# A three-layer graph network with max aggregation on one core: five heavy units for six, distances on ScalarE, the leaky relu on GpSimd, and three middle tiles that pick an edge per pair of source tiles

## The chip, the cores and the metric

The kernel runs on one core of a Trainium2 chip. The time is device time in microseconds for one execution. The profile names the engines PE (TensorE), DVE (VectorE), ACT (ScalarE), POOL (GpSimd) and SP (SyncE, which only issues DMAs here); PEld is TensorE's weight load.

## The reference

`x` has 6250 rows of 128 values, and 200000 edges go from `src` to `dst`, sorted by `dst`. Low node numbers get many edges and high ones few, since `dst` is 6250 times the square of a uniform number. Three SAGE layers of widths 128, 256, 256 take the maximum over incoming edges:

```
def _sage_conv(x, src, dst, Wl, bl, Wr):
    agg = segment_max(x[src], dst, num_segments=x.shape[0])
    agg = where(isfinite(agg), agg, 0.0)
    return agg @ Wl + bl + x @ Wr

h = maximum(_layernorm(x), 0.0)
h = leaky_relu(_sage_conv(h, src, dst, Wl1, bl1, Wr1), 0.01)
h = leaky_relu(_sage_conv(h, src, dst, Wl2, bl2, Wr2), 0.01)
h = leaky_relu(_sage_conv(h, src, dst, Wl3, bl3, Wr3), 0.01)
out = x + h
```

## The kernel before, in words

Nodes are cut into 50 tiles of 127 rows, 25 pairs of source tiles. An edge is aggregated in one of two ways.

The first is a one-hot product. For a destination row and a pair of source tiles, one edge is picked, ScalarE makes a one-hot matrix from the row number (`one_hot`), and TensorE multiplies the pair's rows by it (`products`, line 1002), each row as two halves that add up to it. VectorE takes the maximum into `acc` (`maxima`, line 1026). A light unit ("n") picks one edge per pair, and its two source tiles go into one product and one maximum. The other units ("m", "w", and the heavy units' second set "x") pick one edge per source tile, which means two products and two maxima (the code calls such a step `alone`, or `odd`). A step is 1024 columns in layer 0 and 512 in layers 1 and 2. The units form five groups, each with a plane of 128 columns per unit: 24 light tiles, 11 middle tiles (11 to 21), the heavy rows (tiles 0 to 2, cut into `NV` units of rows with at most `CUT_V` edges, followed by their second set), 8 wide tiles and 4 more light ones. `STARTS` says at which pair of a layer each group enters; in layers 1 and 2 the light and the heavy group take part from pair 0 to 24, the middle one from 10 to 34, the wide one from 19, and the last four from 28.

The second way is for edges that are left over. They are sorted by list length, and `Listed.gather` fetches a row per list place by an indirect DMA on GpSimd (line 1064), followed by a pause, a `memset` of 300 columns (`gap_t`, line 1068). VectorE takes maxima over the gathered tiles (lines 1079 and 1084) some steps later. `CAPS` holds how long each list is.

What is picked is worked out in layer 0, beside its products. `expand` finds, for each row and each source tile, the smallest edge: five distances by an exclusive or (line 772), a tree of minima (line 778) and a reduction, all on VectorE. Each is one chore of `late_lookups`; the chores are spread over the steps of layer 0 by their cost.

When a tile's products and lists are done, `Node` runs it in stages on later steps: `fetch` (GpSimd, line 1118), `merge`, `linear` (TensorE into `z_p`, then ScalarE copies `z_p` to `s`, line 1151), `rows` (VectorE's leaky relu into `h`, lines 1158 and 1162, and the write to the next layer's table), `turn` (TensorE transposes `h` into `hT_p`, line 908; ScalarE rounds `h` into `pr`) and `rest` (`keep_halves`: VectorE subtracts, line 918). In layer 0 such a tile starts every step, in layer 1 and 2 every second step for the light and middle tiles.

The order is written out by hand: a loop over steps `t` issues what `agenda` holds for the step, in ranks. Each engine runs its instructions in that order.

Of the kernel before, what the change touches and what calls it, by code (L numbers as in the profile page):

```python
# [32 lines left out]
F32 = mybir.dt.float32  # L33
# [3 lines left out]
I16 = mybir.dt.int16  # L37
# [17 lines left out]
LEAF = 1 << 14  # L55
VT, NV, CUT_V = 3, 6, 96
CAPS = (
    (13, 11, 10, 9, 8, 8, 7, 7, 6, 6, 6, 6, 5, 5, 5, 4, 4, 4, 3, 3, 3, 2, 2, 1),
    (26, 22, 18, 13, 9, 5),
    (14, 11, 10, 8, 7, 7, 6, 5, 4, 4, 3),  # L60
    (33, 24, 20, 17, 15, 13, 11, 9),
    (14, 10, 8, 6),
)
# [7 lines left out]
FIRST = 24  # L71
PAUSE = 300


@with_exitstack
def kernel(ctx: ExitStack, tc: tile.TileContext, x, src, dst,
# [15 lines left out]
    widths = (D, H, H)  # L92
    PAST = NG << 8
    assert NT * P <= PAST and PAST + NT * P < LEAF


    WIDE = list(range(VT, 11))
    NARROW = list(range(26, NT)) + list(range(22, 26))
    MIDDLE = list(range(11, 22))
    NW, NN, NM = len(WIDE), len(NARROW), len(MIDDLE)  # L100
    VIRT = 2
    GROUPS = (
        [("n", i) for i in range(24)],
        [("m", i) for i in range(NM)],
        [("w", NW + v) for v in range(NV)],
# [426 lines left out]
    def flag_rows(us, S):  # L532
# [45 lines left out]
    def pick_rows(k, i0, us, S):  # L578
# [186 lines left out]

    def expand(us, J, g0, s, least, S):

        n = len(us)
        r = rows_of(us)
        t = S(0, I16, BATCH * n, J).rearrange("p (i u) j -> p i u j", i=BATCH)  # L770
        for i in range(BATCH):
            nc.vector.tensor_scalar(
                t[:, i, :, :], r[:, :, :J], ((g0 + i) << 8) | (s << 7), None, op0=OP.bitwise_xor
            )
        w = J
        while w % 4 == 0 and w > 8:
            w //= 2
            nc.vector.tensor_tensor(t[:, :, :, :w], t[:, :, :, :w], t[:, :, :, w : 2 * w], op=OP.min)
# [4 lines left out]
    turns = itertools.cycle(("tr", "z"))  # L783
    stored = [0] * len(GROUPS)

    def lookups(us, least, s, pool, tags=("v", "v8")):

        n = len(us)
        wide = us[0][0] != "n"
        v = pool.tile([P, n, NG], BF16, tag=tags[0], name="v", bufs=1 + (tags[0] == "v"))  # L790
        nc.vector.scalar_tensor_tensor(v, least, float(P if wide else 2 * P), least, op0=OP.is_lt, op1=OP.mult)
        v8 = pool.tile([NG, n * P], U8, tag=tags[1], name="v8")
        i = 0
        while i < n:
# [107 lines left out]
    def halves(layer, a, h):  # L902
# [11 lines left out]
        return pr  # L914

    def keep_halves(layer, a, h, pr):
        F = widths[layer]
        nc.vector.tensor_sub(pr[:, 1, :F], h[:, :F], pr[:, 0, :F].bitcast(F32))
        nc.sync.dma_start(pairs[layer][a // 2][:, a % 2, :, :], pr[:, :, :F].bitcast(F32))
# [109 lines left out]
    class Listed:  # L1029
# [25 lines left out]
        def gather(self, t):  # L1055
# [11 lines left out]
            )  # L1067
            nc.gpsimd.memset(gap_t, 0.0)  # L1068

# [30 lines left out]
    class Node:  # L1100
# [41 lines left out]
        def linear(self):  # L1142
# [7 lines left out]
            self.s = s = node.tile([P, H], F32, tag="s", name="s", bufs=2)  # L1150
            nc.scalar.copy(s[:R, :FO], z_p[:R, :])  # L1151

        def rows(self):
            layer, a, FO, s = self.layer, self.a, self.FO, self.s
            if layer < 2:
                self.h = h = h_ts[turn_h[0] % len(h_ts)]
                turn_h[0] += 1
                nc.vector.scalar_tensor_tensor(h[:R, :FO], s[:R, :FO], SLOPE, s[:R, :FO], op0=OP.mult, op1=OP.max)  # L1158
# [3 lines left out]
            nc.vector.scalar_tensor_tensor(s[:R, :FO], s[:R, :FO], SLOPE, s[:R, :FO], op0=OP.mult, op1=OP.max)  # L1162
# [124 lines left out]
    def late_lookups(us, s):  # L1287
        got = {}
        for g0 in range(0, NG, BATCH):
# [5 lines left out]
        chores.append((2, lambda: lookups(us, got[0], s, made)))  # L1295

# [478 lines left out]
```

## Time and profile before

| | us |
|---|---|
| runs, median of 3 | 3166.22 (3161.16 to 3170.59) |
| profiled execution | 3162.05 |
| its span, first to last instruction | 3160.2 |
| busy: VectorE | 2717.8 (86%) |
| busy: GpSimd | 2430.8 (77%) |
| busy: TensorE | 2332.1 (74%) |
| busy: ScalarE | 1433.9 (45%) |

A group of instructions in the profile is told as: line, engine, operation, output<-input, shapes, count | busy us, mean ns of one | idle us of the engine just before them <- what ended it. A wait is told as: who waited <- for what: us in total, times, longest. DMA-issuing and register instructions are not counted as busy, and "issue" is time in which an engine waited for nothing that the profile shows.

### The profile page before, as it was taken

Reading aid. Unit: us, or ns where it says so; the run is one execution under the profiler, and the core shown is the slowest. Engines: PE = TensorE matmul, PEld = TensorE weight load, DVE = VectorE, ACT = ScalarE, POOL = GpSimd, SP = SyncE. Lnnn points to the kernel's source line nnn. Section 1 sums busy time; section 2 is a strip of 40 time slices with the busy share of each in tenths; the row PEclk is TensorE's granted clock in tenths of the full one; section 3 lists DMA queues with packets and bytes.
Section 4 is the critical chain, followed back from the end, with each engine's and each line's share of the span. In section 5 each row is a group of like instructions: output and inputs, shape, how many; then the busy total and the mean of one; then the engine's idle time right before and its main releaser. Section 6 shows DMA issues by size and latency. Waiting matters only on the chain.

```text
span 3160.2 us, 37328 instructions
## 1 busy us (share of the span) xinstructions
PE 2332.1 (74%) x9394; PEld 1710.8 (54%) x9394; DVE 2717.8 (86%) x4441; ACT 1433.9 (45%) x2394; POOL 2430.8 (77%) x3424
## 2 busy tenths in 40 slices
PE   1024554456566778899888878889999988888997
PEld 1023333334344455677666656666676666666665
DVE  6668988987898975999999988876799999998995
ACT  5214443333544666555454434444555545443342
POOL 6666888688778883888888786763688888788882
PEclk9996766777767999999999999999999999999998
DMA  9322334266645797556454456778455554555675
GB/s 259 116 65 82 116 111 115 80 179 215 197 156 174 221 270 243 160 157 189 144 153 151 149 162 217 235 217 265 155 172 162 174 141 156 157 153 174 201 221 153
DMA packets 303458, 538.58 MB, mean 170 GB/s; under 512 B 57245, under 2 KB 165589, under 8 KB 302595
## 3 DMA queue, kind: packets, MB, share of 16 engines
q1 hardware_dynamic: 206573, 302.97, 29.7%
q0 software_dynamic: 78592, 196.07, 23.0%
q10 hardware_dynamic: 18070, 37.07, 3.1%
q8 instruction: 79, 1.29, 0.2%
q14 instruction: 144, 1.18, 0.1%
HBM read 409.84 MB, written 126.04 MB: 170 GB/s over the span
## 4 chain that ended last, share of the span: by engine, by line
DVE 19%; PE 16%; POOL 12%; DMA 6%; issue 6%; ACT 1%; SPq 0%; DVEq 0%; POOLq 0%; ACTq 0%
DVE acc L1026 13%; PE pg L1002 11%; POOL g L1064 8%; DMA g<-table,let 4%; POOL gap_t L1068 3%; DVE g L1079 2%; DVE g L1084 2%; PE z_p L1147 2%; PE z_p L1149 1%; DMA out_dram<-s 1%; DMA pair_sb<-pair 1%; ACT hot L985 0%; DMA agg_v<-best,end_i 0%; PE hT_p L908 0%; DMA xt<-in_x_dram 0%
## 5 line engine op out<-in xcount | busy, mean ns | idle before, releaser
L1002 PE MATMUL pg<-hot,pair_sb 128*128 128x512 f32 (+1 forms) x7500 | 2036.3, 421 | 414.2 <-DVE acc L1026 241.3
L1002 PEld LDWEIGHTS pg<-hot,pair_sb 128*128 128x128 f32 x7500 | 1436.1, 202 | 873.4 <-issue 285.9
L1064 POOL DMA_INDIRECT g<-table,let x1518 | 1523.9, 1004 | 492.6 <-issue 237.6
L1026 DVE TENSOR_TENSOR acc<-acc,pg 128x1024 f32<-128x1024 f32 (+4 forms) x1614 | 1663.6, 1057 | 207.1 <-PE pg L1002 164.7
L985 ACT ACTIVATE hot<-idx_sb 128x1024 fp32r<-128x1024 uint8 (+2 forms) x1050 | 909.6, 886 | 714.0 <-PE pg L1002 548.5
L1068 POOL MEMSET gap_t<- 128x300 f32 x1518 | 566.5, 373 | 0.7
L983 ACT ACTIVATE hot<-idx_sb,last_b 128x1024 fp32r<-128x1024 int8 (+1 forms) x300 | 310.3, 1034 | 37.2 <-PE pg L1002 24.9
L1118 POOL DMA_INDIRECT agg<-best,end_i x141 | 140.1, 994 | 104.1 <-PE aT_p L1134 60.5
L1151 ACT COPY s<-z_p 127x256 f32<-127x256 f32 (+1 forms) x150 | 50.4, 336 | 363.2 <-PE z_p L1149 325.8
L1079 DVE TENSOR_TENSOR g<-g 128x1024 f32<-128x1024 f32 (+6 forms) x214 | 207.8, 971 | 0.3
L1084 DVE TENSOR_TENSOR g<-g 128x256 f32<-128x256 f32 (+3 forms) x377 | 183.2, 487 | 11.2 <-issue 0.2
L1147 PE MATMUL z_p<-wr,hT_in 128*128 128x256 f32 (+1 forms) x500 | 138.7, 395 | 0.6 <-DMA hT_in<-across 0.6
L1149 PE MATMUL z_p<-wl,mz 128*128 128x256 f32 (+1 forms) x500 | 121.4, 360 | 11.9 <-DVE mz L1140 11.9
L908 PE MATMUL hT_p<-ident,h 128*128 128x128 f32 x200 | 44.3, 306 | 88.2 <-DVE h L1158 82.0
L973 DVE TENSOR_SCALAR idx_sb<-idx_sb,own_b 128x512 int32<-128x512 int32 (+3 forms) x125 | 73.4, 588 | 35.8 <-DMA idx_sb<-idx 30.6
L910 ACT COPY hT<-hT_p 128x254 f32<-128x254 f32 x100 | 37.1, 371 | 145.8 <-PE hT_p L908 129.0
L1149 PEld LDWEIGHTS z_p<-wl,mz 128*128 128x128 f32 x500 | 89.5, 204 | 25.1 <-DVE mz L1140 14.9
L652 POOL DMA_INDIRECT picks<-picked,to_i x53 | 61.5, 1161 | 48.2 <-DVE rank_f L629 23.5
L1140 DVE TENSOR_TENSOR mz<-acc,aT_p 128x256 f32<-128x256 f32 (+1 forms) x141 | 52.4, 371 | 53.3 <-PE aT_p L1134 53.3
L1147 PEld LDWEIGHTS z_p<-wr,hT_in 128*128 128x128 f32 x500 | 80.7, 203 | 31.7 <-issue 13.3
L908 PEld LDWEIGHTS hT_p<-ident,h 128*128 128x128 f32 x200 | 24.1, 149 | 120.1 <-issue 54.9
L806 ACT CAST v<-lk_p 25x1024 uint8<-25x1024 bf16 (+4 forms) x16 | 11.5, 747 | 165.7 <-PE lk_p L804 165.7
(291 smaller groups left out, 1298.0 us busy)
## 6 DMA issues: line engine op xcount, KB each, us to landing
pair_sb<-pair SPq DMA_DIRECT2D x106, 512.0 KB
idx_sb<-far SPq DMA_DIRECT2D x100, 384.0 KB
pair<-pr SPq DMA_DIRECT2D x100, 256.0 KB
g<-table,let POOLq DMA_INDIRECT x1518
pair_sb<-pair SPq DMA_DIRECT2D x85, 256.0 KB
idx_sb<-idx SPq DMA_DIRECT2D x50, 384.0 KB
far<-idx_sb ACTq DMA_DIRECT2D x50, 384.0 KB
idx_sb<-far SPq DMA_DIRECT2D x50, 352.0 KB
```

The lines of the kernel that those rows point to most:

```text
L973: nc.vector.tensor_scalar(words, words, own_b.bitcast(I32)[:, 0:1], None, op0=OP.bitwise_xor)
L983: nc.scalar.activation(hot[:, :w], far_b.bitcast(I8), AF.Relu, bias=last_b, scale=-1.0)
L985: nc.scalar.activation(hot[:, :w], far_b, AF.Relu, bias=1.0, scale=-1.0)
L1002: nc.tensor.matmul(to, pr[:, s, i, kk * P : (kk + 1) * P], hot[:, o : o + bw], start=((alone or s == 0) and i == 0), stop=((alone or s == ...
L1026: nc.vector.tensor_max(to, to, of)
L1064: nc.gpsimd.indirect_dma_start(out=self.tiles[q, b][:, i, :], out_offset=None, in_=tables[self.layer], in_offset=bass.IndirectOffsetOnAxis ...
L1068: nc.gpsimd.memset(gap_t, 0.0)
L1079: nc.vector.tensor_max(base[:, : i + 1, :], base[:, : i + 1, :], g[:, : i + 1, :])
L1084: nc.vector.tensor_max(base[:, :h, :], base[:, :h, :], base[:, w - h : w, :])
L1118: nc.gpsimd.indirect_dma_start(out=self.agg[:, : self.F], out_offset=None, in_=of, in_offset=bass.IndirectOffsetOnAxis(ap=at, axis=0),)
L1147: nc.tensor.matmul(z_p, self.hT[:, i, :], wr[layer][:, i, :], start=False, stop=False)
L1149: nc.tensor.matmul(z_p, self.m[:, i, :], wl[layer][:, i, :], start=False, stop=(i == K - 1))
```

## The change

- The heavy rows form five units of up to 104 edges instead of six of up to 96, so their plane has 10 places instead of 12.
- Tiles 19 to 21 become light units that stay in the middle group's plane, behind its other eight.
- A source node's number becomes 256 x tile + row (it was 128 x tile + row in effect, as node number plus tile). For all but light units the five distances are then ScalarE's `Abs` with a bias (`keys`), issued one chore ahead of the minima, in four scratch areas in turn. Light units keep VectorE's exclusive or. Two small operations per pick bring the number back.
- `CAPS` holds other list lengths, 487 places in all instead of 490.
- ScalarE computes relu(z) into `s` and relu(-0.01 z) into `h`, and GpSimd subtracts them (`in_place`). The subtraction of `keep_halves` is GpSimd's too. For each of these, the next two gathers go without their pause.

The diff, cut to its core:

```diff
+FAR = 2 * P
-VT, NV, CUT_V = 3, 6, 96
+VT, NV, CUT_V = 3, 5, 104
 CAPS = (
-    (13, 11, 10, 9, 8, 8, 7, 7, 6, 6, 6, 6, 5, 5, 5, 4, 4, 4, 3, 3, 3, 2, 2, 1),
...
+    (13, 11, 10, 9, 8, 8, 7, 7, 6, 6, 6, 5, 5, 5, 4, 4, 4, 4, 3, 3, 2, 2, 1, 1),
...
+SPARE = 2
-    NARROW = list(range(26, NT)) + list(range(22, 26))
-    MIDDLE = list(range(11, 22))
+    NARROW = list(range(26, NT)) + list(range(22, 26)) + list(range(19, 22))
+    MIDDLE = list(range(11, 19))
...
-        [("m", i) for i in range(NM)],
+        [("m", i) for i in range(NM)] + [("n", i) for i in range(28, NN)],
...
-    nc.vector.scalar_tensor_tensor(scol, c_i, 1.0, srci, op0=OP.add, op1=OP.add)
+    nc.vector.tensor_scalar(c_i, c_i, float(FAR - R), 1.0, op0=OP.mult, op1=OP.add)
+    nc.vector.tensor_tensor(scol, c_i, srci, op=OP.add)
...
-        nc.vector.tensor_scalar(picked[k][:, i0 : i0 + n, :], top, -float(LEAF), 0.0, op0=OP.add, op1=OP.max)
+        pick, off = picked[k][:, i0 : i0 + n, :], S(1, I16, n, m)
+        nc.vector.tensor_scalar(pick, top, -float(LEAF), 0.0, op0=OP.add, op1=OP.max)
+        nc.vector.tensor_scalar(off, pick, 1.0 / FAR, -0.499, op0=OP.mult, op1=OP.add)
+        nc.vector.scalar_tensor_tensor(pick, off, -float(FAR - P), pick, op0=OP.mult, op1=OP.add)
...
-    def expand(us, J, g0, s, least, S):
+    def expand(us, J, g0, s, S, area=0):
         n = len(us)
         r = rows_of(us)
-        t = S(0, I16, BATCH * n, J).rearrange("p (i u) j -> p i u j", i=BATCH)
+        wide = us[0][0] != "n"
+        t = S(area, I16, BATCH * n, J).rearrange("p (i u) j -> p i u j", i=BATCH)
         for i in range(BATCH):
-            nc.vector.tensor_scalar(
-                t[:, i, :, :], r[:, :, :J], ((g0 + i) << 8) | (s << 7), None, op0=OP.bitwise_xor
-            )
+            a = 2 * (g0 + i) + s
+            if wide:
+                nc.scalar.activation(t[:, i, :, :], r[:, :, :J], AF.Abs, bias=keys[:, a : a + 1], scale=1.0)
+            else:
+                nc.vector.tensor_scalar(t[:, i, :, :], r[:, :, :J], a * FAR, None, op0=OP.bitwise_xor)
+        return t
+
+    def shrink(t, us, J, g0, least):
...
+    paused = [0]
+
+    def in_place(out, a, b):
+        nc.gpsimd.tensor_tensor(out, a, b, op=OP.subtract)
+        paused[0] += SPARE
+
     def keep_halves(layer, a, h, pr):
         F = widths[layer]
-        nc.vector.tensor_sub(pr[:, 1, :F], h[:, :F], pr[:, 0, :F].bitcast(F32))
+        in_place(pr[:, 1, :F], h[:, :F], pr[:, 0, :F].bitcast(F32))
...
-            nc.gpsimd.memset(gap_t, 0.0)
+            if paused[0]:
+                paused[0] -= 1
+            else:
+                nc.gpsimd.memset(gap_t, 0.0)
...
-            nc.scalar.copy(s[:R, :FO], z_p[:R, :])
+            self.h = b = h_ts[turn_h[0] % len(h_ts)]
+            turn_h[0] += 1
+            nc.scalar.activation(s[:R, :FO], z_p[:R, :], AF.Relu)
+            nc.scalar.activation(b[:R, :FO], z_p[:R, :], AF.Relu, scale=-SLOPE)
...
-                nc.vector.scalar_tensor_tensor(h[:R, :FO], s[:R, :FO], SLOPE, s[:R, :FO], op0=OP.mult, op1=OP.max)
+                in_place(h[:R, :FO], s[:R, :FO], h[:R, :FO])
...
-            nc.vector.scalar_tensor_tensor(s[:R, :FO], s[:R, :FO], SLOPE, s[:R, :FO], op0=OP.mult, op1=OP.max)
+            in_place(s[:R, :FO], s[:R, :FO], h[:R, :FO])
...
                 if g0 == 0:
-                    got[0] = made.tile([P, len(us), NG], I16, tag="least", name="least", bufs=2)
-                expand(us, slots_of(us), g0, s, got[0], S_acc)
+                    got["least"] = made.tile([P, len(us), NG], I16, tag="least", name="least", bufs=2)
+                    got[0] = expand(us, J, 0, s, S_acc, next(areas))
+                if g0 + BATCH < NG:
+                    got[g0 + BATCH] = expand(us, J, g0 + BATCH, s, S_acc, next(areas))
+                shrink(got.pop(g0), us, J, g0, got["least"])
...
-        late_lookups(GROUPS[1], s)
+        late_lookups(GROUPS[1][:NM], s)
+    late_lookups(GROUPS[1][NM:], 0)
```

Three places show how instructions move. The first is VectorE's queue in layer 1, one pair of source tiles in which the light, the middle and the heavy group take part (`acc_1500` and `acc_1505` hold the light group, `acc_1501` and `acc_1506` the others). Before:

```order
L1026 TENSOR_TENSOR acc_1501<-acc_1501,pg 128x2x512 x5
L1026 TENSOR_TENSOR acc_1501<-acc_1501,pg 128x2x256 x4
L1026 TENSOR_TENSOR acc_1500<-acc_1500,pg 128x2x512 x2
L1026 TENSOR_TENSOR acc_1501<-acc_1501,pg 128x2x384
L1079 TENSOR_TENSOR g<-g 128x1024
L1026 TENSOR_TENSOR acc_1501<-acc_1501,pg 128x2x384
L1026 TENSOR_TENSOR acc_1501<-acc_1501,pg 128x2x512 x2
```

The same place in the changed kernel:

```order
L1054 TENSOR_TENSOR acc_1506<-acc_1506,pg 128x2x512
L1054 TENSOR_TENSOR acc_1506<-acc_1506,pg 128x2x128
L1054 TENSOR_TENSOR acc_1506<-acc_1506,pg 128x2x384
L1054 TENSOR_TENSOR acc_1506<-acc_1506,pg 128x2x128
L1054 TENSOR_TENSOR acc_1506<-acc_1506,pg 128x2x384
L1054 TENSOR_TENSOR acc_1505<-acc_1505,pg 128x2x512
L1110 TENSOR_TENSOR g<-g 128x1024
L1054 TENSOR_TENSOR acc_1505<-acc_1505,pg 128x2x512
L1054 TENSOR_TENSOR acc_1506<-acc_1506,pg 128x2x384
L1054 TENSOR_TENSOR acc_1506<-acc_1506,pg 128x2x256 x2
```

The three tiles' 384 columns come once instead of twice, and the heavy group's last maxima are 2x256 instead of 2x512; its other part splits as 128 and 384 instead of 256 and 256.

The second is VectorE's queue in layer 0, one chore that looks up the heavy units. Before, with the distances (L772) ahead of the tree:

```order
L772 TENSOR_SCALAR acc_1500<-rows_w 128x576 x5
L778 TENSOR_TENSOR acc_1500<-acc_1500 128x30x48
L778 TENSOR_TENSOR acc_1500<-acc_1500 128x30x24
L778 TENSOR_TENSOR acc_1500<-acc_1500 128x30x12
L778 TENSOR_TENSOR acc_1500<-acc_1500 128x30x6
L779 TENSOR_REDUCE least<-acc_1500 128x5x6
```

In the changed kernel the distances stand on ScalarE's queue, between one-hots (L1011, L1013) and the numbers for gathers (L1081):

```order
L1470 DMA far_158<-idx_sb 128x3072
L783 ACTIVATE acc_1505<-rows_w,keys 128x520 x10
L1011 ACTIVATE hot<-idx_sb,last_b 128x1024
L1081 ACTIVATE let<-ell_852 128x1
L1013 ACTIVATE hot<-idx_sb 128x1024
L783 ACTIVATE acc_1506<-rows_w,keys 128x520 x5
```

and VectorE's queue has, for the first of these chores:

```order
L1001 TENSOR_SCALAR idx_sb<-idx_sb,own_b 128x768
L793 TENSOR_TENSOR acc_1505<-acc_1505 128x25x52
L793 TENSOR_TENSOR acc_1505<-acc_1505 128x25x26
L794 TENSOR_REDUCE least<-acc_1505 128x5x5
L1115 TENSOR_TENSOR g<-g 128x384
```

Five distances and two minima left VectorE's queue per chore; the first lookup of a kind puts ten distances in a row on ScalarE's.

The third is GpSimd's queue in layer 0 while a tile's stages run each step. Before:

```order
L1118 DMA agg<-best_0_140,end_i_861 128x128
L1064 DMA g<-table_75,let 128x128
L1068 MEMSET gap_t 128x300
L1064 DMA g<-table_75,let 128x128
L1068 MEMSET gap_t 128x300
L1064 DMA g<-table_75,let 128x128
L1068 MEMSET gap_t 128x300
```

In the changed kernel:

```order
L1149 DMA agg<-best_0_140,end_i_862 128x128
L941 TENSOR_TENSOR h_1484<-s,h_1484 127x256
L941 TENSOR_TENSOR pr<-h_1483,pr 128x256
L1092 DMA g<-table_75,let 128x128 x3
L1149 DMA agg<-best_0_140,end_i_862 128x128
```

The pauses are gone and two subtractions stand ahead of the step's gathers. In layer 0, 130 gathers go without a pause; the first 70 gathers of layer 1 and the first 82 of layer 2 do so too, on what the layer before left over.

More of the change, by code (lines that the diff above doesn't have):

```diff
@@ L55 @@
 LEAF = 1 << 14
-VT, NV, CUT_V = 3, 6, 96
+VT, NV, CUT_V = 3, 5, 104
 CAPS = (
-    (13, 11, 10, 9, 8, 8, 7, 7, 6, 6, 6, 6, 5, 5, 5, 4, 4, 4, 3, 3, 3, 2, 2, 1),
[L59 to L62, printed above, removed]
+    (13, 11, 10, 9, 8, 8, 7, 7, 6, 6, 6, 5, 5, 5, 4, 4, 4, 4, 3, 3, 2, 2, 1, 1),
+    (29, 23, 18, 13, 9),
+    (16, 12, 11, 10, 9, 8, 7, 6, 5, 5, 3),
+    (30, 23, 19, 16, 14, 12, 10, 8),
+    (14, 10, 8, 5),
 )
@@ L92 @@
     widths = (D, H, H)
-    PAST = NG << 8
-    assert NT * P <= PAST and PAST + NT * P < LEAF
+    PAST = NG * 2 * FAR
+    assert NT * FAR <= PAST < LEAF and LEAF + PAST < 1 << 15
     WIDE = list(range(VT, 11))
-    NARROW = list(range(26, NT)) + list(range(22, 26))
-    MIDDLE = list(range(11, 22))
+    NARROW = list(range(26, NT)) + list(range(22, 26)) + list(range(19, 22))
+    MIDDLE = list(range(11, 19))
     NW, NN, NM = len(WIDE), len(NARROW), len(MIDDLE)
@@ L109 @@
     EXTRA = [("x", v) for v in range(NV)]
-    PLANES = [units + (EXTRA[4:] + EXTRA[:4] if k == VIRT else []) for k, units in enumerate(GROUPS)]
+    EC = (2 * NV) % 4
+    assert 4 < NV < 8 and 2 * NV - EC == 8
+    PLANES = [units + (EXTRA[EC:] + EXTRA[:EC] if k == VIRT else []) for k, units in enumerate(GROUPS)]
     STARTS = ((0, 40, 25, 53, 60), (0, 10, 0, 19, 28), (0, 10, 0, 19, 28))
@@ L541, in flag_rows @@
             nc.vector.tensor_copy(ri, r[:, :, :J])
-            nc.vector.tensor_scalar(g, ri, 8, None, op0=OP.arith_shift_right)
+            nc.vector.tensor_scalar(g, ri, 9, None, op0=OP.arith_shift_right)
             nc.vector.tensor_tensor(b, one[:, None, :].to_broadcast([P, n, J]), g, op=OP.logical_shift_left)
-            nc.vector.tensor_scalar(o, ri, 24, 31, op0=OP.logical_shift_left, op1=OP.arith_shift_right)
+            nc.vector.tensor_scalar(o, ri, 23, 31, op0=OP.logical_shift_left, op1=OP.arith_shift_right)
             nc.vector.tensor_tensor(o, o, b, op=OP.bitwise_and)
@@ L552, in flag_rows @@
             g, seen = (S(i, I32, n, J) for i in (1, 1))
-            nc.vector.tensor_scalar(g, r[:, :, :J], 1.0 / 256, -0.499, op0=OP.mult, op1=OP.add)
+            nc.vector.tensor_scalar(g, r[:, :, :J], 1.0 / (2 * FAR), -0.499, op0=OP.mult, op1=OP.add)
             nc.vector.tensor_tensor(b, one[:, None, :].to_broadcast([P, n, J]), g, op=OP.logical_shift_left)
@@ L783 @@
     turns = itertools.cycle(("tr", "z"))
+    areas = itertools.cycle(range(4))
+    keys = keep.tile([P, NT], F32, name="keys")
+    nc.vector.tensor_scalar(keys, iota_f[:, :NT], -float(FAR), None, op0=OP.mult)
     stored = [0] * len(GROUPS)
@@ L789, in lookups @@
         wide = us[0][0] != "n"
+        if not wide:
+            less = pool.tile([P, n, NG], I16, tag=tags[0] + "_less", name="less")
+            nc.vector.tensor_scalar(less, least, float(FAR), float(P - FAR), op0=OP.is_ge, op1=OP.mult)
+            nc.vector.tensor_add(least, least, less)
         v = pool.tile([P, n, NG], BF16, tag=tags[0], name="v", bufs=1 + (tags[0] == "v"))
@@ L799, in lookups @@
             if us[i] in EXTRA:
-                m = min(m, 4 - us[i][1] % 4)
+                m = min(m, (EC if us[i][1] < EC else NV) - us[i][1])
             at = PLANES[k].index(us[i]) + (len(PLANES[k]) if s else 0)
@@ L886 @@
     for g0 in range(0, NG, BATCH):
-        expand(L0, CB, g0, 0, least, S_first)
+        shrink(expand(L0, CB, g0, 0, S_first), L0, CB, g0, least)
     next(rest_v, None)
@@ L1150, in linear @@
             self.s = s = node.tile([P, H], F32, tag="s", name="s", bufs=2)
-            nc.scalar.copy(s[:R, :FO], z_p[:R, :])
+            self.h = b = h_ts[turn_h[0] % len(h_ts)]
+            turn_h[0] += 1
+            nc.scalar.activation(s[:R, :FO], z_p[:R, :], AF.Relu)
+            nc.scalar.activation(b[:R, :FO], z_p[:R, :], AF.Relu, scale=-SLOPE)
         def rows(self):
-            layer, a, FO, s = self.layer, self.a, self.FO, self.s
+            layer, a, FO, s, h = self.layer, self.a, self.FO, self.s, self.h
             if layer < 2:
-                self.h = h = h_ts[turn_h[0] % len(h_ts)]
-                turn_h[0] += 1
-                nc.vector.scalar_tensor_tensor(h[:R, :FO], s[:R, :FO], SLOPE, s[:R, :FO], op0=OP.mult, op1=OP.max)
+                in_place(h[:R, :FO], s[:R, :FO], h[:R, :FO])
                 nc.sync.dma_start(tables[layer + 1][1 + a * P : 1 + (a + 1) * P, :], h)
@@ L1270, in late_rows @@
         i0 = 0
-        for part in (us,):
+        for _, part in itertools.groupby(us, key=lambda u: u[0]):
+            part = list(part)
             chores.append((2.5, lambda part=part: mask_rows(part, S_acc)))
@@ L1288, in late_lookups @@
         got = {}
+        J = slots_of(us)
         for g0 in range(0, NG, BATCH):
@@ L1291, in part @@
                 if g0 == 0:
-                    got[0] = made.tile([P, len(us), NG], I16, tag="least", name="least", bufs=2)
-                expand(us, slots_of(us), g0, s, got[0], S_acc)
+                    got["least"] = made.tile([P, len(us), NG], I16, tag="least", name="least", bufs=2)
[3 more added lines that the diff above has]
+                shrink(got.pop(g0), us, J, g0, got["least"])
             chores.append((.7 * len(us), part))
-        chores.append((2, lambda: lookups(us, got[0], s, made)))
+        chores.append((2, lambda: lookups(us, got["least"], s, made)))
     stops = []
```

## The prediction

> **What bounds the kernel now.** I read the page's first lines, then the busy times by stage, then who waits for whom inside the long stages, and last the groups of instructions by form.
>
> ```profile
> span 3160.2 us, 37328 instructions
> PE 2332.1 (74%) x9394; PEld 1710.8 (54%) x9394; DVE 2717.8 (86%) x4441; ACT 1433.9 (45%) x2394; POOL 2430.8 (77%) x3424
> ```
>
> No engine fills the span, so the average decides nothing. The cut into stages does (stretch and its length, then busy us of PE, PEld, DVE, ACT and POOL with instruction counts, then the granted clock, DMA share and GB/s):
>
> ```profile
> 0.00:229.00 229.00, 31.70 (x140) 25.31 (x140) 149.13 (x618) 62.48 (x143) 146.65 (x168) 1.00 0.49 142
> 229.00:402.00 173.00, 87.49 (x284) 65.35 (x284) 156.98 (x398) 80.17 (x107) 131.50 (x193) 0.73 0.34 104
> 402.00:629.00 227.00, 110.03 (x351) 81.28 (x352) 206.34 (x476) 88.32 (x124) 184.90 (x267) 0.70 0.37 105
> 629.00:822.00 193.00, 116.68 (x396) 76.49 (x394) 159.06 (x336) 73.01 (x158) 161.01 (x224) 0.76 0.65 198
> 822.00:986.00 164.00, 103.43 (x298) 70.88 (x298) 152.55 (x323) 77.82 (x127) 131.50 (x188) 0.72 0.56 168
> 986.00:1216.00 230.00, 170.78 (x611) 111.50 (x609) 182.63 (x292) 137.68 (x243) 179.69 (x250) 0.88 0.78 233
> 1216.00:1850.00 634.00, 568.31 (x2319) 422.62 (x2320) 581.00 (x639) 331.33 (x493) 522.35 (x765) 0.98 0.53 163
> 1850.00:2201.00 351.00, 302.29 (x1342) 227.42 (x1341) 276.86 (x355) 142.59 (x298) 225.90 (x306) 0.97 0.71 223
> 2201.00:2835.00 634.00, 571.77 (x2338) 423.37 (x2337) 581.42 (x634) 330.54 (x488) 522.27 (x766) 0.99 0.52 160
> 2835.00:3160.00 325.00, 269.61 (x1324) 206.60 (x1322) 271.79 (x378) 109.91 (x218) 225.07 (x304) 0.93 0.63 189
> ```
>
> The first row is the setup, the next five are layer 0, then come layers 1 and 2, each cut where the 24 light tiles' matmuls end (1850, 2835). VectorE is the fullest engine in layer 0 until 986, except from 629 to 822, and in the long halves of layers 1 and 2 (581 of 634 us, 92%). After 1850 TensorE is (302 of 351). GpSimd looks free and is not: half its instructions are gathers, and each costs issue time that is not counted as busy.
>
> ```profile
> L1064 POOL DMA_INDIRECT g<-table,let x1518 | 1523.9, 1004 | 492.6 <-issue 237.6 <-ACT let L1053 162.5 <-DMA across<-hT 27.6
> L1068 POOL MEMSET gap_t<- 128x300 f32 x1518 | 566.5, 373 | 0.7
> L1118 POOL DMA_INDIRECT agg<-best,end_i x141 | 140.1, 994 | 104.1 <-PE aT_p L1134 60.5 <-issue 16.0 <-DMA pair_sb<-pair 11.1
> ```
>
> A gather with its pause costs 1.00 + 0.37 + 237.6/1518 = 1.53 us. The 380 of 1216 to 1850 take 582 of 634 us. With the 27.6 us wait for the table at a layer's start, GpSimd has about 25 us to spare there. So VectorE is first, GpSimd close behind, TensorE third (568). The waits from 1264 to 1820 agree:
>
> ```profile
> PE pg L1002 <- DVE acc L1026: 44.0, 61, 2.4
> POOL g L1064 <- ACT let L1053: 12.2, 8, 7.6
> DVE acc L1026 <- PE pg L1002: 11.7, 19, 1.9
> ```
>
> TensorE waits four times as long for the maxima as VectorE for the products, and GpSimd hardly waits.
>
> **The change, part by part.** VectorE's rows:
>
> ```profile
> L1026 DVE TENSOR_TENSOR acc<-acc,pg 128x1024 f32<-128x1024 f32 x1096 | 1305.9, 1216 | 149.3 <-PE pg L1002 123.5 <-ACT acc L1024 4.4 <-ACT hot L985 1.3
> L1026 DVE TENSOR_TENSOR acc<-acc,pg 128x512 f32<-128x512 f32 x272 | 186.0, 684 | 15.8 <-PE pg L1002 5.6 <-ACT acc L1024 2.5
> L1026 DVE TENSOR_TENSOR acc<-acc,pg 128x768 f32<-128x768 f32 x147 | 139.7, 950 | 38.0 <-PE pg L1002 35.0
> L1026 DVE TENSOR_TENSOR acc<-acc,pg 128x384 f32<-128x384 f32 x49 | 26.9, 550 | 2.5 <-PE pg L1002 0.7
> L1026 DVE TENSOR_TENSOR acc<-acc,pg 128x256 f32<-128x256 f32 x50 | 21.0, 420 | 1.7
> L1158 DVE SCALAR_TENSOR_TENSOR h<-s 127x256 f32<-127x256 f32 x100 | 42.1, 421 | 8.8 <-ACT s L1151 4.9 <-DMA table<-h 3.8
> L918 DVE TENSOR_TENSOR pr<-h,pr 128x256 fp32r<-128x256 f32 x100 | 42.0, 420 | 14.0 <-ACT pr L913 13.8
> L1162 DVE SCALAR_TENSOR_TENSOR s<-s 127x128 f32<-127x128 f32 x50 | 14.3, 286 | 6.3 <-ACT s L1151 6.2
> L772 DVE TENSOR_SCALAR acc<-rows_x 128x576 int16<-128x576 int16 x50 | 19.7, 458 | 0.0
> L772 DVE TENSOR_SCALAR acc<-rows_w 128x512 int16<-128x512 int16 x50 | 19.7, 456 | 0.0
> L772 DVE TENSOR_SCALAR acc<-rows_w 128x576 int16<-128x576 int16 x50 | 19.3, 449 | 0.0
> L772 DVE TENSOR_SCALAR acc<-rows_m 128x528 int16<-128x528 int16 x50 | 17.6, 417 | 0.0
> L778 DVE TENSOR_TENSOR acc<-acc 128x660 int16<-128x660 int16 (+7 forms) x150 | 77.6, 518 | 5.2
> ```
>
> Five heavy units: the plane of heavy units has 10 places instead of 12, so its second part is 2 units wide instead of 4. In layers 1 and 2 that makes 50 maxima of 1024 elements into 512: 50 x (1.216 - 0.684) = 26.6 us a layer; in layer 0, 50 x (0.684 - 0.420) = 13.2. The first part only splits elsewhere. TensorE saves half of 200 matmuls a layer, at 568.31/2319 = 0.245 us each: 24 us.
>
> Pair tiles 19 to 21: their product is one maximum instead of two, 25 fewer a layer: 25 x 0.950 = 23.8 us in layers 1 and 2, 15 x 0.950 = 14 of it before 1850 (2835); 25 x 0.550 = 13.8 in layer 0. TensorE does the same matmuls.
>
> Distances: 76.3 us of L772 leave VectorE in layer 0 (those of the heavy units, 39.0, before 629; the others, 17.6 and 19.7, mostly from there to 822 and half of the last after it). The tree under them loses 30 of 150 instructions of 0.52 us. Against that, the three tiles' own distances stay on VectorE, and each of the ten pick blocks gains two small operations. I set these equal: zero.
>
> Counted lists: 503 gathers a layer instead of 506, under 5 us of GpSimd each: zero.
>
> Relu on GpSimd: 98.4 us leave VectorE (L1158, L918, L1162). GpSimd gets 250 subtractions, and skips the pause of two gathers for each; 485 of 500 skips find a gather. The trace has no GpSimd instruction with two inputs, so I bound it by `gap_t`'s row above and these two:
>
> ```profile
> masks.py:199 POOL TENSOR_SCALAR_AFFINE_SELECT ident<-ident 128x128 f32<-128x128 f32 x1 | 0.3, 292 | 0.1
> masks.py:197 POOL MEMSET ident<- 128x128 f32 x1 | 0.2, 216 | 0.0
> ```
>
> Writing alone costs 0.10 us and 0.91 ns an element (0.216 at 128, 0.373 at 300), so 0.33 us at 256 wide is the lower end. One input costs at most (292 - 100)/128 = 1.5 ns, two inputs in turn 3.0, so 0.87 us is the upper end. I take 0.64 (one more stream on top of 1.5: about 2.1 ns), nearest to the row that reads, and 0.16 for the issue: 0.80. Two skipped pauses return 0.75, so GpSimd's whole is unchanged, but not its place: in the node stages it pays, and 70 and 82 skips are left for the first gathers of layers 1 and 2, worth 26 and 30 us where it is nearly full. The Trainium skill's GPSIMD Engine Reference (section 4.1, Engine selection) says an elementwise operation on two inputs is about twice as slow there as on VectorE; by it one costs 1.96 x 0.42 = 0.82 us, and the sum would be up to 45 us worse; no run here shows it yet.
>
> ScalarE, at 45%, gets 200 distances and a second relu per tile:
>
> ```profile
> L985 ACT ACTIVATE hot<-idx_sb 128x512 fp32r<-128x512 uint8 x225 | 140.5, 629 | 132.6 <-PE pg L1002 123.4 <-DVE idx_sb L973 4.8 <-DMA idx_sb<-far 2.3
> L1151 ACT COPY s<-z_p 127x256 f32<-127x256 f32 x100 | 37.2, 372 | 191.0 <-PE z_p L1149 187.8 <-DMA pair_sb<-pair 1.9 <-DMA hT_in<-across 1.4
> PE hT_p L908 <- DVE h L1158: 82.0, 47, 6.8
> ```
>
> About 0.6 us a distance, 120 us, all in layer 0, where it is busy 457 of 987 us. The distances are queued a block of five ahead of their minimum. Only the first block of each of eight lookups is exposed, 3 us at most, often under the maxima ahead: 0 to 24 us, I take 8. Behind them stand one-hots, of which TensorE has three steps in hand.
>
> Now by stage. 229 to 629: VectorE loses 39 of 363 us; GpSimd, 316 busy and about 35 of issue, is then the fuller, with 351 of 400: 25. 629 to 822, 24 tiles at one per step: VectorE loses about 43 of 159 (25 of distances, 20 of relu and `pr`, 8 of maxima, less 10 for the three tiles' own distances), but GpSimd has 161 + 20 = 181 of 193 us, 48 x 0.80 = 38 come and about 62 x 0.37 = 23 go, so it binds: 8. 822 to 986: VectorE loses 10 of distances, 10 x 0.53 + 12 x 0.55 = 12 of maxima, and 36 pauses go: 18. 986 to 1216: VectorE at 79%, GpSimd gains load: 5. Layer 0 together 56. 1216 to 1850: VectorE loses 26.6 + 14 = 41, GpSimd 26, TensorE 24: I take 30, between GpSimd's and VectorE's. 1850 to 2201: VectorE loses 42 + 9.5, but TensorE sets the pace: 10. 2201 to 2835: 31. The rest: VectorE loses 24, GpSimd is as full as before: 7. Setup: the column code is one operation longer, 1 back. The end of layers 0 and 1, where each tile's next step is serial: the extra relu (0.37) and the slower subtraction, 0.7 us for 12 tiles, 8 back in all, since part lies beside matmuls.
>
> Sum, with the 8 for exposed distances: -56 - 30 - 10 - 31 - 7 + 1 + 8 + 8 = -117. The profiled execution took 3162.05 us (span 3160.2), 4 below the median of the runs, 3166.22: 3162 - 117 = 3045.
>
> **Rivals.** VectorE alone binds, and what it loses comes off in full where it is above 90%: 39 + 22 in layer 0 with half of the 43 between, 41 in each of layers 1 and 2, and 20 of the last 24: 185, less the 17 of costs, 168: 2994. For it: TensorE waits for the maxima. Against: GpSimd's 582 of 634.
>
> GpSimd takes over as the bound: the subtraction costs the upper end, 0.87, and collides with list maxima: 250 x 0.23 = 58 us more, and layer 0 gives only the stretch after 822: 3045 + 58 + 25 = 3128. The Trainium skill's SBUF — State Buffer (section Who interferes with whom) says that a VectorE instruction with two SBUF inputs and a GpSimd instruction that reads SBUF exclude each other; no run here shows it, GpSimd's memset only writes.
>
> Slower: the transposes of a new row block on TensorE (`hT_p`, 82.0 us of waits now) wait for a subtraction that stands in GpSimd's queue behind gathers. One gather in front costs 1.16 us; 100 transposes behind one gather and the other subtraction, 1.16 + 0.80, are 196 us, so 3241. It decides from 1.2 us of added wait per transposed tile (117/100). Against: the subtraction stands ahead of its own step's gathers, and GpSimd runs only two or three gathers a step.
>
> **How the numbers follow.** The forecast 0.48 (3010 to 3100), VectorE alone 0.22 (2960 to 3010), GpSimd the bound 0.21 (3100 to 3165), slower 0.09. The range, 2970 to 3125, leaves out about 0.04 below and 0.16 above. A difference under 0.3% (9.5 us) cannot be told from none here: faster 0.86, same 0.05, slower 0.09.
>
> **What the profile after would show.** L1026 with 75 fewer instructions and about 128 us less; no L772 for heavy rows; VectorE near 2718 - 128 - 98 - 76 = 2416 us busy; subtractions at 0.64 us; GpSimd's share up; 1216 to 1850's stretch near 604. Wrong would be a subtraction above 0.87, TensorE's wait for `h` above 120 us, VectorE waiting for gathers or distances, or a layer 0 that shortens by more than 90.

## The result: 16.6 times slower, because one row out of 6250 has three left-over edges too many

The changed kernel took 52596.19 us (median of 4, 52579.38 to 52643.66) against 3165.24 before: a ratio of 16.62, 95% interval 16.59 to 16.65. Forecast were 3045 (2970 to 3125). First the head of its page, then its time in two stretches (length, busy us of PE, PEld, DVE, ACT and POOL with instruction counts, granted clock, DMA share, GB/s), then two of its groups.

```profile
span 52594.1 us, 574099 instructions
```

```profile
0.00:3059.60 3059.60, 2278.48 (x9371) 1692.40 (x9371) 2459.07 (x3930) 1553.05 (x2734) 2401.08 (x3174) 0.91 0.56 172
3059.60:52594.10 49534.50, 4906.88 (x14364) 3252.29 (x14364) 8465.65 (x44642) 173.30 (x539) 6107.02 (x6445) 0.50 0.07 22
```

```profile
L1721 POOL DMA_INDIRECT g_g<-g_table,g_i x4719 | 4455.6, 944 | 28374.8 <-PEq L1715 28232.0
...
L1639 POOL DMA_INDIRECT g_sorted<-g_pair,g_pos x1573 | 1506.6, 958 | 14405.1 <-DVEq L1615 9840.7
```

The first 3059.6 us are the kernel that the prediction is about. What follows are instructions that the run before never issues: 574099 in all, for 37328. Names that begin with `g_` belong to a second program in the same kernel, the end of which reads:

```
    general = nc.values_load(falls_i[0:1, 0:1], min_val=0, max_val=1)
    with tc.If(general > 0):
        general_path(...)
```

The kernel is planned for a certain shape of the edge lists. On the way it counts where the input breaks the plan (the edges unsorted, a list longer than `CAPS` allows, too many heavy rows, a window too narrow), and if any count is above zero, `general_path` computes everything again, one gather at a time: 4719 loops of (4455.6 + 28374.8)/4719 = 6.96 us and 1573 of (1506.6 + 14405.1)/1573 = 10.1 us, which are 48.7 of the 49.5 ms.

The plan allows a row only so many left-over edges. `DEEP` gives the middle list 24 columns, and the last has to stay empty, so 23 are allowed. Counting the edges of the input by the kernel's rules shows the row: node 2764, in tile 21, with 42 incoming edges. By one pick per source tile 16 of them are left over. By one pick per pair of source tiles (and from the first 32 edges, not 48) 26 are. With the pairs but still the first 48 edges 23 would be, which fits: the three too many come with the shorter reach. The change gave tiles 19 to 21 the second rule and left `DEEP` as it was. Before, the list's deepest row had 19.

### The profile page after: what moved, and what is told of

Same layout as the page of the kernel before. It is cut to its first block, busy times and chain, and to the rows that moved or that the text cites. A ratio compares the mean times of both kernels' runs of the same rounds, so it can differ in the third digit from the quotient of the medians.

```text
span 52594.1 us, 574099 instructions
## 1 busy us (share of the span) xinstructions
PE 7185.4 (14%) x23735; PEld 4944.7 (9%) x23735; DVE 10924.7 (21%) x48572; ACT 1726.4 (3%) x3273; POOL 8508.1 (16%) x9619
## 5 line engine op out<-in xcount | busy, mean ns | idle before, releaser
L1721 POOL DMA_INDIRECT g_g<-g_table,g_i x4719 | 4455.6, 944 | 28374.8 <-PEq L1715 28232.0
L1725 DVE SCALAR_TENSOR_TENSOR g_state<-g_state,g_m,g_g 128x256 f32<-128x256 f32 (+1 forms) x4719 | 2076.7, 440 | 14973.0 <-DMA g_g<-g_table,g_i 14973.0
L1639 POOL DMA_INDIRECT g_sorted<-g_pair,g_pos x1573 | 1506.6, 958 | 14405.1 <-DVEq L1615 9840.7
L1605 PE MATMUL g_count<-g_oa_t,g_ob_t 128*128 128x49 f32 x6292 | 2041.7, 425 | 3651.7 <-DVE g_ob_t L1600 3552.1
L1030 PE MATMUL pg<-hot,pair_sb 128*128 128x512 f32 (+2 forms) x7500 | 1981.1, 413 | 414.3 <-DVE acc L1054 179.8
L1605 PEld LDWEIGHTS g_count<-g_oa_t,g_ob_t 128*128 128x128 f32 x6292 | 1578.8, 312 | 4322.6 <-issue 3760.7
L1054 DVE TENSOR_TENSOR acc<-acc,pg 128x1024 f32<-128x1024 f32 (+5 forms) x1539 | 1541.5, 1026 | 305.5 <-PE pg L1030 266.0
L1627 PE MATMUL g_at_p<-g_nxt,g_obT 128*128 128x49 f32 x3146 | 1044.1, 432 | 603.3 <-DVE g_obT L1625 603.3
L1600 DVE TENSOR_SCALAR g_ob_t<-iota_f,g_ab_t 128x128 f32<-128x128 f32 x3146 | 878.3, 279 | 0.0
L1013 ACT ACTIVATE hot<-idx_sb 128x1024 fp32r<-128x1024 uint8 (+3 forms) x975 | 839.5, 881 | 644.7 <-PE pg L1030 489.1
```

The source lines that it names most:

```text
L1013: nc.scalar.activation(hot[:, :w], far_b, AF.Relu, bias=1.0, scale=-1.0)
L1030: nc.tensor.matmul(to, pr[:, s, i, kk * P : (kk + 1) * P], hot[:, o : o + bw], start=((alone or s == 0) and i == 0), stop=((alone or s == ...
L1054: nc.vector.tensor_max(to, to, of)
L1600: nc.vector.tensor_scalar(ob, iota_f, c[:, 1:2], None, op0=OP.is_equal)
L1605: nc.tensor.matmul(p, ob, oa, start=True, stop=True)
L1627: nc.tensor.matmul(at_p, obT, nxt, start=True, stop=True)
```

## Which condition fires, and what the planned part is worth

The runs came in three groups of four, each on one chip with its own runs of the kernel before. The chips differ (before took 3237.25, 3163.37 and 3242.47 us), so only ratios and runs of one group are compared.

### Eleven conditions, each with its own mark

In place of the general path stands one `memset` for each condition, 8 columns wider each time, so that the width in the trace names the condition. This kernel leaves the general path out.

```diff
-    general = nc.values_load(falls_i[0:1, 0:1], min_val=0, max_val=1)
-    with tc.If(general > 0):
-        general_path(...)
+    for i in range(NL + 6):
+        general = nc.values_load(falls_i[0:1, i : i + 1], min_val=0, max_val=1)
+        with tc.If(general > 0):
+            nc.vector.memset(mark[:, : 8 * (i + 1)], 0.0)
```

> The changed kernel, and in place of the general path one small memset for each of the eleven conditions (two of the sort order, five lists, heavy rows, three windows), so the trace tells which of them fires. The general path is left out. Theory A: only the condition of the middle list, memset of 40 columns... the fifth of the eleven. Theory B: the heavy list's (fourth), or several. The time is that of the planned part in both, 3063 to 3075 with eleven branches.

The rows of the tile `mark` in the trace, first of this kernel, then of the one with 32 columns in the middle list and six further conditions (a row with at least 20, 23, 24, 25, 26, 27 edges left):

> The same with 32 columns in the middle list, and six further conditions: at least one row of the middle list has 20, 23, 24, 25, 26 or 27 edges left. The general path is left out. Theory A: none of the first eleven fires, and of the six those for 20 to 26 do and 27 does not: five memsets. Theory B: one or more of the first eleven. Time as the run with 32 columns, 10 to 20 us more for the branches.

```profile
L1543 DVE MEMSET mark<- x1: 92/92/92, 3174.0 to 3174.0; 128x40 f32 x1
```

```profile
L1547 DVE MEMSET mark<- x5: 138/152/165, 3162.1 to 3165.2; 128x96 f32 x1, 128x104 f32 x1, 128x112 f32 x1, 128x120 f32 x1
...
3165.16 0.17 DVE L1547 MEMSET mark<- 128x128 f32 x1 [0.51 <-DVE mark L1547]
```

One mark of 40 columns: the fifth condition, the middle list, and no other. With 32 columns the first eleven are silent, and five of the six marks are there, from 96 columns on (the row lists four forms and counts five; the last line, in order of time, is the fifth). The one for 27 is missing: the deepest row has 26. The heavy units, which fill 637 of their 640 rows, do not fire, and neither does their list. Theory A is shown, theory B is out. The first took 3183.59 us, for 3063 to 3075 expected, and the second 3171.57, on a chip where the kernel before takes 3237.

### The change with a list deep enough

```diff
-DEEP = (24, 40, 24, 48, 24)
+DEEP = (24, 40, 32, 48, 24)
```

> The changed kernel with DEEP[2] = 32 for 24: the middle list may hold 32 places per row. Theory A (one row too deep): counted on the edges, the pair picks of tiles 19 to 21 leave 26 edges at one row, and the list has 24 columns, so the check at the end sends the whole kernel through the general path after the planned one. With 32 columns nothing is over: the planned part of the changed kernel ended at 3059.5 us of the span, 1.9 us lie around it, so 3061, at most 5 more for the longer ranking; 0.967 of before. Theory B (a list's counted places are too few, such as the heavy list, 637 rows for 640 places): more depth does not help, 52.6 ms again.

> The run with 32 columns once more, as the base of this group: 0.981 of before if this is a chip like the one of the group before (3177 for 3237), 0.967 if it is like the first (3061 for 3165). In the first group its pairs 1 to 9 of layers 1 and 2 took 198 us each where the planned part of the changed kernel took 175 on the first chip, with VectorE and ScalarE waiting for something that no record shows.

> The run with 32 columns again, as the base of this group: 0.969 of before on a chip like the one of the second group (3062 for 3163), 0.981 on one like that of the first.

Measured: 3176.84 for 3237.25 (0.981, 0.9769 to 0.9851), 3062.2 for 3163.37 (0.969, 0.9656 to 0.9724), 3173.8 for 3242.47 (0.9775, 0.9727 to 0.9823). One number takes 49.5 ms away, and the change is then faster than before on every chip, by 1.9, 3.1 and 2.3%; only the second interval lies wholly beyond 2%. The 0.967 expected of the first run was missed, and the second run came out at 0.969. Against the kernel before, no complete kernel of this study has a lower median, though the relu's in the table below comes close. In the second group the kernel before takes what it took beside the result (3163 and 3165), so its run is read from here on as "the base":

```profile
span 3062.1 us, 36923 instructions
...
PE 2274.7 (74%) x9371; PEld 1687.0 (55%) x9371; DVE 2466.9 (81%) x3963; ACT 1551.8 (51%) x2734; POOL 2402.3 (78%) x3174
```

### Tiles 19 to 21 back in the middle group

```diff
-    NARROW = list(range(26, NT)) + list(range(22, 26)) + list(range(19, 22))
-    MIDDLE = list(range(11, 19))
+    NARROW = list(range(26, NT)) + list(range(22, 26))
+    MIDDLE = list(range(11, 22))
```

with the middle list's old lengths in `CAPS`, and `DEEP` left at 24.

> The changed kernel with tiles 19 to 21 back in the middle group, an edge per source tile (and that list's old lengths, 79 places for 92), DEEP[2] = 24 as before. Theory A: the deepest row of that list has 19 left, so the general path is not taken; 75 maxima come back (61 us of VectorE) and 39 gathers go (58 us of GpSimd). If VectorE sets the pace, 40 to 60 us above the run with 32 columns: 3100 to 3120; if GpSimd does, as fast or up to 40 faster: 3020 to 3060. Theory B, with the heavy list: 52.6 ms still, since that list is the changed one.

3218.7 (0.9933, 0.9906 to 0.9959). No general path: without the pair picks the 24 columns do, which shows from the other side that these picks overran them. Against the 32-column run of its group it is 42 us slower, though its lists have 39 gathers less, as expected if VectorE sets the pace. In the traces 26 us of it lie in pairs 0 to 24 of each of layers 1 and 2, where the three tiles' second maxima are back. That these cost the time is likely and not shown, since the picks and the lists changed with them.

### Pauses, relu with its pauses, heavy units, distances, undone in turn

```diff
# pauses
-SPARE = 2
+SPARE = 0
# relu back (the subtraction of the halves likewise)
-            nc.scalar.activation(s[:R, :FO], z_p[:R, :], AF.Relu)
-            nc.scalar.activation(b[:R, :FO], z_p[:R, :], AF.Relu, scale=-SLOPE)
+            nc.scalar.copy(s[:R, :FO], z_p[:R, :])
-                in_place(h[:R, :FO], s[:R, :FO], h[:R, :FO])
+                nc.vector.scalar_tensor_tensor(h[:R, :FO], s[:R, :FO], SLOPE, s[:R, :FO], op0=OP.mult, op1=OP.max)
# six heavy units (with that list's old lengths)
-VT, NV, CUT_V = 3, 5, 104
+VT, NV, CUT_V = 3, 6, 96
# distances back
-            if wide:
-                nc.scalar.activation(t[:, i, :, :], r[:, :, :J], AF.Abs, bias=keys[:, a : a + 1], scale=1.0)
-            else:
+            if True:
```

> 32 columns, and every gather keeps its pause (SPARE = 0); the subtractions stay on GpSimd. 476 pauses come back; a gather behind a gather starts after 0.30 us, one behind a pause after 0.37 + 0.16, so GpSimd gets 476 x 0.23 = 110 us more. Theory G (GpSimd's time is what the stages wait for): 30 to 70 us slower than the base. Theory D (gathers without pauses hold up other transfers, above all in pairs 1 to 9 of layers 1 and 2): 10 to 50 us faster, and pairs 1 to 9 come back to 170 to 175 us. Neither: within 10.

> 32 columns, with the leaky relu and the subtraction of the halves back on VectorE, one copy of z on ScalarE, and every pause kept. VectorE +98 us, GpSimd -250 x (0.77 + 0.16) + 476 x 0.23 = -122 us. If VectorE sets the pace: 30 to 80 us slower than the base. If GpSimd and its gathers do: 20 to 60 faster. The prediction's sum (70 of 98 us gained by the move, half of it through skipped pauses) says 40 to 60 slower.

> 32 columns, with six heavy units of up to 96 edges again (and that list's old lengths). 50 maxima a layer go from 512 to 1024 columns: VectorE +26.6 us in layers 1 and 2 and +13.2 in layer 0, TensorE +24 us a layer, and 39 us of distances more on ScalarE. If the two set the pace of the first half of layers 1 and 2: 50 to 65 us slower than the base. If that half waits for gathers or transfers, as its gain of 6 for a forecast 30 us hints: 0 to 30 slower.

> 32 columns, with all distances back on VectorE (the exclusive or, as the light units have it). VectorE gets some 76 us back in layer 0, ScalarE loses 200 x 0.68 = 136 us. If VectorE sets layer 0's pace until its step 52: 25 to 50 us slower than the base, all of it ahead of layer 1. If GpSimd or TensorE does, or the distances on ScalarE hold up the one-hots behind them: within 10 us or faster.

| undone in the 32-column run | us, ratio to before (95%) | against its base |
|---|---|---|
| pauses kept | 3121.48, 0.9874 (0.9849 to 0.9899) | +59 |
| relu and halves on VectorE, pauses kept | 3073.14, 0.9715 (0.9693 to 0.9737) | +11 |
| six heavy units | 3102.67, 0.982 (0.9794 to 0.9847) | +40 |
| distances on VectorE | 3195.64, 0.986 (0.9808 to 0.9912) | +22 |

The relu's interval overlaps the base's, and the distances' just touches that of its own base: the first is at most a small gain, the second a likely one. Only the pauses fell where a theory had them (G, 30 to 70). The relu's 11 lies outside every case, the heavy units' 40 between the two, and the distances' 22 just under 25 to 50; in the traces it does lie ahead of layer 1. The surprise is the pair of the first two rows. Moving the relu to GpSimd without skipping pauses makes the kernel 48 us slower than not moving it (3121 for 3073). The skipped pauses earn 59, and 11 remain. By stage, from the first matmul of a source-tile pair to that of another, us ("forecast, got" is the change from before to the base):

| stretch | before | base | forecast, got | pauses | relu back | six |
|---|---|---|---|---|---|---|
| layer 0, pairs 0 to 24 | 404.4 | 383.0 | -25, -21 | 385.7 | 386.3 | 397.8 |
| pairs 25 to 39 | 191.2 | 188.2 | -8, -3 | 197.3 | 174.0 | 186.2 |
| pairs 40 to 51 | 161.4 | 150.7 | -18, -11 | 159.5 | 152.6 | 155.1 |
| pair 52 to layer 1 | 230.0 | 232.1 | -5, +2 | 233.7 | 227.9 | 228.3 |
| layer 1, pairs 0 to 24 | 634.5 | 625.6 | -30, -9 | 630.2 | 621.0 | 627.7 |
| pair 25 to layer 2 | 350.6 | 323.8 | -10, -27 | 344.3 | 353.0 | 331.8 |
| layer 2, pairs 0 to 24 | 633.9 | 615.2 | -31, -19 | 615.1 | 618.8 | 625.7 |
| the rest | 325.0 | 313.5 | -7, -12 | 322.3 | 313.4 | 312.9 |

In pairs 25 to 39 the relu on GpSimd costs 14 us, skipped pauses and all. From pair 25 to layer 2 the move alone gains 9 us (344, for 353 with the relu on VectorE and every pause kept), and the skipped pauses 20 more (324).

### Fewer pauses still

```diff
# no pause after the first subtraction
-SPARE = 2
+SPARE = 100
# relu on VectorE, a pause before every second gather
-            if paused[0]:
-                paused[0] -= 1
-            else:
+            paused[0] += 1
+            if paused[0] % 2:
                 nc.gpsimd.memset(gap_t, 0.0)
```

> 32 columns, relu on GpSimd as in the change, and no gather waits for a pause. GpSimd gets 1033 x 0.23 = 238 us less than the base. Theory G: 40 to 100 us faster than the base, 2960 to 3020 on a chip like that of the second group. Rival (the pauses keep other transfers moving): the pair and row transfers wait behind gathers, 20 us slower or more, or no gain.

> 32 columns, relu and halves on VectorE as in the run with both back (3073 for 3163, 0.9715), and a pause before every second gather only. GpSimd gets 755 x 0.23 = 174 us less than in that run. The run with every pause showed 59 us for 110 us of GpSimd; at that rate 3073 - 93 = 2980, by half of it 3027. Theory G (GpSimd's load is what the stages wait for): 2980 to 3030 on such a chip, 0.942 to 0.957, faster than both kernels. Rival V (with the relu on VectorE that engine sets the pace again): 3060 to 3075, 0.967 to 0.972.

Both are far slower than before: 3385.18 (1.044, 1.0391 to 1.0489) and 3370.11 (1.0411, 1.0377 to 1.0445), 211 and 196 us above the base of their group. Theory G's extrapolation is wrong, and so is rival V; the rival that had the pauses keep other transfers moving has the sign right. In the traces the kernel without pauses loses 66 and 91 us in pairs 0 to 24 of layers 1 and 2, and nothing from pair 25 to layer 2, where the base's gathers skip most pauses too. Waits of the base of that group, then of the kernel without pauses (who waited <- for what: us, times, longest):

```profile
POOL g L1092 <- ACT let L1081: 140.2, 48, 20.3
PE pg L1030 <- issue: 115.5, 73, 17.8
DVE acc L1054 <- remote: 50.4, 10, 12.8
```

```profile
POOL g L1092 <- ACT let L1081: 366.6, 81, 20.3
PE pg L1030 <- issue: 216.0, 129, 18.4
DVE acc L1054 <- remote: 141.9, 47, 10.7
```

TensorE and VectorE both wait longer for something that no record shows ("issue" and "remote"), and GpSimd, with less to do, waits for the one-hots' engine. Transfers on the other queues held up by gathers would look like this, but no row names them, so what the pauses protect stays open. That leaving most of them out costs time is shown.

In the two groups on the other chips pairs 1 to 9 of layers 1 and 2 of the 32-column run, where the 70 and 82 gathers without pauses stand, took 198 us each, and 175 and 171 on the base's chip. There the run that kept every pause took 177 and 171, so on that chip these skips cost nothing; on the others no such run was made.

## Why the prediction was wrong, step by step

**The step that failed** is "Counted lists: 503 gathers a layer instead of 506, under 5 us of GpSimd each: zero". It priced how long the lists are and not how deep one may be, and no rival had the change leave the plan it is written for. In place of that zero the runs showed 49.5 ms, from one row of 26 in a list that holds 23. No profile of before could show it, since the general path does not run there. The kernel's text and the edges of the input do: the count that found node 2764 needs neither chip nor trace. Of the forecast, 0.86 lay on faster, and the 0.09 on slower stood for another mechanism.

**The planned part** came out at 3062 in the base, against the forecast's 3045: its sum of -117 was -101 for 3163. Term by term:

The subtractions and the distances, base:

```profile
L941 POOL TENSOR_TENSOR pr<-h,pr 128x256 fp32r<-128x256 f32 x100 | 77.4, 774 | 39.4 <-ACT pr L935 36.7 <-PE z_p L1176 1.8
L941 POOL TENSOR_TENSOR h<-s,h 127x256 f32<-127x256 f32 x100 | 76.3, 763 | 45.2 <-ACT h L1185 39.0 <-DMA across<-hT 2.4 <-DMA hT_in<-across 2.4
...
L783 ACT ACTIVATE acc<-rows_w,keys 128x520 int16<-128x520 int16 x50 | 31.7, 713 | 5.1 <-DVE acc L624 5.1
...
L941 POOL TENSOR_TENSOR s<-s,h 127x128 f32<-127x128 f32 x50 | 24.6, 493 | 39.8 <-ACT h L1185 35.3 <-DVE acc L1054 2.5 <-ACT let L1081 1.5
```

- A subtraction costs 0.77 us, inside the bounds 0.33 to 0.87, above the 0.64 taken; that is 0.77/0.42 = 1.8 times VectorE's time. The Trainium skill's GPSIMD Engine Reference (section 4.1, Engine selection), which says about twice and by which the estimate was 0.82, was the better guide.
- "Two skipped pauses return 0.75" is mis-sized. A gather straight behind a gather starts 0.30 us after it, and behind a pause 0.16 us after the pause. The two places in the changed kernel's order of time (start, duration, idle ahead):

```profile
1279.24 0.95 POOL L1092 DMA_INDIRECT g<-table,let  x1 [0.30 <-issue]
1280.49 0.95 POOL L1092 DMA_INDIRECT g<-table,let  x1 [0.30 <-issue]
...
1334.00 0.95 POOL L1092 DMA_INDIRECT g<-table,let  x1 [0.16 <-issue]
1334.95 0.37 POOL L1099 MEMSET gap_t<- 128x300 f32 x1
1335.48 0.95 POOL L1092 DMA_INDIRECT g<-table,let  x1 [0.16 <-issue]
```

  So a skip between two gathers saves 1.48 - 1.25 = 0.23 us, and two return 0.46 for the 0.77 that a subtraction costs. In all the 250 subtractions take 178 us, and the 476 skips that found a gather (485 were reckoned) return about 110, where the prediction had GpSimd's whole unchanged.
- The wait that the move adds was not priced. GpSimd stood idle ahead of its subtractions until ScalarE had made `h` or `pr`, with the gathers queued behind: 39.0 + 36.7 + 35.3 = 111 us, the releasers in the rows above. The "slower" rival looked for this wait on TensorE, where it shrank: `hT_p` waits 42.7 us for `h`, for 82.0 before. On the other side its gathers wait less for their row numbers (`let`), 79.9 us in all for 162.5 before. These waits and the skip's true price are a likely reason why a move that takes 98 us off VectorE is worth 11, but no run separates them.
- Maxima: 75 instructions fewer and 122 us less, for 75 and 128 forecast. The largest form keeps its time, 1216 ns:

```profile
L1054 DVE TENSOR_TENSOR acc<-acc,pg 128x1024 f32<-128x1024 f32 x996 | 1188.1, 1216 | 199.4 <-PE pg L1030 178.9 <-ACT acc L1052 2.1 <-ACT hot L1013 1.2
```

  So these maxima, which read `acc` from SBUF and `pg` from PSUM, were not slowed by GpSimd's subtractions. With two SBUF inputs the 1024-wide list maxima went from 1.221 to 1.230 us, and the subtractions' means lie 0.02 to 0.04 us above their medians (longest 1.53), about 8 us in all. The second rival's collision of 58 us did not come. The Trainium skill's SBUF — State Buffer (section Who interferes with whom) has an instruction of VectorE with two SBUF inputs contend with GpSimd's reads; if it happened here, it is within these few us.
- Distances take 0.60 to 0.71 us each, but they overlap, and the 200 keep ScalarE busy for 121 us, as forecast (120). VectorE waits 19.2 us for them (forecast 8, at most 24). VectorE lost 251 us in all, for 302 forecast (2466.9 instead of 2416).
- "TensorE saves half of 200 matmuls a layer", 24 us, is near: the products are 7500 matmuls in both traces, and 200 in each of layers 1 and 2 became 256 columns wide. In pairs 0 to 24 TensorE's busy time fell by 17 and 22 us.
- In the second rival the sum leaves out the stretch from 629 to 822: 3045 + 58 + 25 + 8 is 3136, not 3128, which still lies in that rival's 3100 to 3165.

The long halves of layers 1 and 2 gave 9 and 19 us for 30 and 31. In layer 1, VectorE fell there from 581 of 634 us to 537 of 626 (the first row is that stretch, the second the one behind it, the third the first stretch with six heavy units, the fourth a wait of the base's GpSimd in it):

```profile
1184.00:1809.60 625.60, 550.96 (x2323) 413.96 (x2323) 536.73 (x603) 324.19 (x501) 504.59 (x713) 0.98 0.53 162
1809.60:2133.40 323.80, 300.75 (x1338) 227.80 (x1336) 239.28 (x256) 154.19 (x339) 243.65 (x266) 0.96 0.76 239
...
1198.10:1825.80 627.70, 570.81 (x2322) 424.42 (x2323) 561.82 (x604) 335.02 (x500) 507.31 (x713) 0.98 0.53 163
...
POOL g L1092 <- issue: 64.7, 321, 4.0
```

The next bound was close. Six units give TensorE 20 and VectorE 25 us more to do there, and the stretch gets 2 us longer (627.7); with the relu back on VectorE it is 621.0. So neither of the two sets its pace. GpSimd, whose gathers also cost issue time, has 504.6 + 64.7 = 569 of 626 us and is the fullest. That would fit, but no run shows it. Pairs 0 to 9 of layer 1 even took 9 us more than before in the base and 4 to 12 more in the three variants of its group, which share most of the new list lengths; those alone were not tried. The second row is where the forecast was too low, 27 for 10. The prediction read TensorE as the pace there; but with the same matmuls in three runs the stretch took 353, 344 and 324 us, so TensorE had room. GpSimd's gathers waited there for their row numbers from ScalarE, before and in the run with the relu back on VectorE:

```profile
POOL g L1064 <- ACT let L1053: 66.3, 21, 9.6
...
POOL g L1092 <- ACT let L1081: 67.9, 23, 6.9
```

In the base that wait is gone. What ends it was not tried alone.

So the likeliest case, 3010 to 3100, held the planned part, for reasons that were half right and with some luck: layer 0 and the two long halves gave 56 us less than forecast, the other stretches 21 more, and 17 of costs had been set against the gains. The kernel was 49.5 ms late for a reason that was not looked for.

## What to carry to other kernels

Before pricing a change to a planned kernel, find what decides whether the plan is used at all, and count the input against every limit the change touches. A rule that looks at fewer edges and picks fewer does not only lengthen a list, it deepens its worst row, and here 3 edges in 200000 cost a factor of 16. Work moved to a nearly full in-order engine is paid for by what stands behind it: here 98 us off one engine, with the pauses skipped for it, came to 11 on the clock. And a pause that looks like waste may be worth its time: skipping 476 of 1509 gained 59 us, and on another chip skipping 1274 took 211 us more than skipping 476.

## What was not expected of the hardware

- GpSimd starts a gather 0.30 us after a gather, and 0.16 us after a memset of 300 columns, so a 0.37 us pause between two gathers costs 0.23.
- Gathers nearly all without pauses (235 left of 1509) made a kernel with less work 1.044 times as long as before, with the waits on two other engines put down to nothing that the profile records.
- A two-input subtraction on GpSimd took 0.493 us at 128 columns and 0.774 at 256: 2.2 ns an element and 0.21 us, near the 2.1 ns that the prediction put together, with twice its fixed part.
- The granted clock read 0.50 throughout the general path, in which TensorE is busy 4907 of 49534 us, and 0.91 over the planned part of the same run.
